# An attention block with a gated mixture layer on one core: the first tile's chain re-ordered, and the last unit's queries taken in wide pieces

## The chip, the cores and the metric

The kernel runs on one core of a Trainium2 chip. The metric is the device time of one execution in microseconds (us). The core's engines run side by side and wait for each other by semaphores: TensorE (PE in the profile; PEld is its weight load), VectorE (DVE), ScalarE (ACT), GpSimd (POOL) and SyncE (SP, which here issues nearly all DMAs).

## The reference

All tensors are float32; x is (2, 1024, 512).

```python
xn = (x - mean(x)) / sqrt(var(x) + 1e-5)
q, k, v = xn @ Wq.T + bq, xn @ Wk.T + bk, xn @ Wv.T + bv      # 32 heads of 16
att = softmax(where(causal, q k^T / 4, -inf))
s = (att @ v) @ Wo.T + bo
logits = xn @ W_gate.T                                        # 8 experts, the best 2 kept
h = (xn @ A^T) * route_w                                      # 8 experts of rank 16
g = silu(xn @ W_base.T + b_base + delta(h, B))
out = x + s * g
```

## The kernel before, in words

**Units and steps.** Attention is cut into 16 units (b, oc, c): a batch b of 2, a group oc of 8 heads of 4, a chunk c of 512 queries of 2. A unit is cut into steps. One step computes 512 columns of scores for four heads at a time: `scores(n)` (L1382) writes two PSUM tiles `s`, one for each pair of heads; two `exp` activations on ACT (L1391) write `pt`; `masked(n)` multiplies the pieces on the causal diagonal by `causal` on DVE; and `values(n)` (L1427) multiplies `pt` with v into the PSUM tiles `av0` and `av1` (`par` 0 and 1, four heads each). A step's pieces are tuples (par, key tile, first query, width, column). There are two `s` tiles of each pair's size in all, so scores(n+1) of a pair wait until the `exp` of that pair in step n has read them. A unit with c = 0 has 5 steps, one with c = 1 has 13, so there are 144 steps; the last unit (1, 3, 1) has steps 131 to 143.

**Order on PE.** For each n PE gets scores(n), values(n-1), and then `fill(n)`: a share of all other matrix work. That work is counted in units of MM = 0.853 us, one pass of 512 columns. The tasks are projections of q and k, of v, the gate and the output (as blocks with seven products instead of eight: `qk_blocks_task`, `block_task`), and routing. All go through the helper `matmul` (L221). The block products are `q` and `p`; the last chunk's output is done plainly as `po` by `whole_task` (4 MM, query tiles 0 to 2), `most_task` (3 MM) and `rest_task` (1 MM) for query tile 3.

**How much a step gets.** `fill(n)` sets `share`: an even part of what is left, or more if a task's due step asks for it. It takes units until the unit's end would pass the share: in an ordinary step it stops when what was taken plus 1/8 MM reaches the share, in a step with a causal piece when it plus 1/2 MM does. Before, the even part aims at step 136 with 16 MM kept for after it (`begin = len(plan) - 8`, `last_work`).

**PSUM for other work.** All projections and all transposes share a pool of two PSUM tiles (`mm_tile`); a new one waits until all readers of an older one are done. Two more hold av.

**The last unit before.** Its query tiles of 128 are done one after the other: `last_steps` lists, for each tile t and each par, all key tiles, and groups these 128-wide pieces by four. A tile's sums are copied (`avs`) as soon as it is through, transposed (`post_tile`, L936, PSUM tile `pt_o`), divided by the softmax's sums on DVE (`rc_last`, `olast`), transposed back (`turn_last`, L966, `pt_y`) and copied to `oT` by ACT (L967). Both transposes go through a list `late`, whose entries PE gets at the end of a fill. Then `whole_task` can run. After step 143: one unit of tile 2's `po`, `pt_o` of par 1 of tile 3, tile 2's last unit, `pt_y` of tile 3, `rest_task`. The DVE operations of `finish_tile` (`y`), of the range test (`fine`) and of the final flag (`count`, `sound`) follow. All engines read `sound` at the very end (`values_load`) to decide on a fallback.

**The first tile chain.** `first_task` handles the first 512 tokens in four tiles of 128: DVE statistics, POOL power, DVE normalization (`x`), four PE transposes (`pt_x`, L320), an ACT copy to `xnT` (L323), and projections `project_first` of q (`pq_first`) and k (`pk_first`, L331). Before it, 12 matmuls on `ident` (L170, `warm`) run, which POOL makes.

Of the kernel before, what the change touches and what calls it, by code (L numbers as in the profile page):

```python
# [80 lines left out]
def direct(ctx, tc, sound, x, wq, wk, wv, wo, wb, wa, wg, wB, bq, bk, bv, bo, bb, out):  # L81
# [81 lines left out]
            nc.sync.dma_start(out=dst, in_=src)  # L163


    ident = cst.tile([P, P], F32, name="ident")
    make_identity(nc, ident)
    warm = ps_mm.tile([P, D], F32, tag="mm", name="warm")
    for n in range(4 * WARM):
        nc.tensor.matmul(  # L170
            warm[:, n % 4 * P : n % 4 * P + P], lhsT=ident, rhs=ident, start=True, stop=True
        )
    b_sb = cst.tile([P, 2 * KC], F32, name="b_sb")
    bq_sb, bk_sb = b_sb[:, 0:KC], b_sb[:, KC : 2 * KC]
# [28 lines left out]
    rc_last = cst.tile([P, 2, TT, 4], F32, name="rc_last")  # L203

    MM = 0.853
    TR = 0.11

# [98 lines left out]
    def first_task():  # L308

        xnT = sb.tile([P, KC, C], F32, tag="xnT", bufs=3, name="xnT_0_0")  # L310
        qT = sb.tile([P, 2, C], F32, tag="qT", bufs=3, name="qT_0_0_0")
        kT = sb.tile([P, C], F32, tag="kT", bufs=4, name="kT_0_0_0")
        xnTs[0, 0], qTs[0, 0, 0], kTs[0, 0, 0] = xnT, qT, kT
        pq = ps_av.tile([P, C], F32, tag="av", name="pq_first")
        pk = ps_av.tile([P, C], F32, tag="av", name="pk_first")

        def turn(t):
            pt = mm_tile("pt_x")
            for k in range(KC):
                nc.tensor.transpose(  # L320
                    pt[:, k * P : (k + 1) * P], first[t][:, k * P : (k + 1) * P], ident
                )
            nc.scalar.copy(  # L323
                xnT[:, :, t * P : (t + 1) * P], pt.rearrange("p (k t) -> p k t", k=KC)
            )
            turned_at[0, 0] = now[0] - 5

        def project_first(ps, w, t):
            cols = slice(t * P, (t + 1) * P)
            for k in range(KC):  # L330
                nc.tensor.matmul(  # L331
                    ps[:, cols], lhsT=w[:, k, :], rhs=xnT[:, k, cols], start=k == 0, stop=k == KC - 1
                )

        def queries(par):
            ve.tensor_scalar(
                qT[:, par], pq, bq_sb[:, 0:1], half[:, par : par + 1], ALU.add, ALU.mult
            )

        def keys(t0, t1):  # L340
            cols = slice(t0 * P, t1 * P)
            nc.scalar.activation(kT[:, cols], pk[:, cols], AF.Identity, bias=bk_sb[:, 0:1])

        def transform(t, s):
            normalize(first[t : t + 1], *s)
            turn(t)

        s0 = yield from statistics(first[0 : 1])
        s1 = yield from statistics(first[1 : 2])
        transform(0, s0)  # L350
        b_ps = mm_tile("b_ps")[:, 0 : 2 * KC]
        nc.tensor.transpose(b_ps, b_rows, ident[0 : 2 * KC, 0 : 2 * KC])
        nc.scalar.copy(b_sb, b_ps)
        s2 = yield from statistics(first[2 : 3])
        transform(1, s1)
        project_first(pq, wqks[0][:, 0:KC], 0)
        s3 = yield from statistics(first[3 : 4])
        transform(2, s2)
        project_first(pk, wqks[0][:, KC:], 0)
        transform(3, s3)  # L360
        room["x"] += 1
        keys(0, 1)
        project_first(pq, wqks[0][:, 0:KC], 1)
        project_first(pq, wqks[0][:, 0:KC], 2)
        project_first(pq, wqks[0][:, 0:KC], TT - 1)
        queries(0)
        queries(1)
        for par in range(2):
            ve.tensor_scalar(bq_half[:, par], bq_sb, half[:, par : par + 1], None, ALU.mult)
        ve.tensor_tensor(b_less, bq_sb, bk_sb, ALU.subtract)  # L370
        project_first(pk, wqks[0][:, KC:], 1)
        yield 6 * MM
        project_first(pk, wqks[0][:, KC:], 2)
        project_first(pk, wqks[0][:, KC:], 3)
        keys(1, TT)
        yield 2 * MM
# [552 lines left out]
        later.append((n + 4 + wait, collect))  # L929
        later.append((n + 6 + wait, finish))  # L930

    def post_tile(b, oc, c, t, pars, avs):

        pt2 = mm_tile("pt_o")[:, 0 : 2 * P].rearrange("p (a s r) -> p a s r", a=2, s=4)
        for a in pars:
            nc.tensor.transpose(  # L936
                pt2[:, a].rearrange("p s r -> p (s r)"), avs[:, a * P : a * P + P], ident
            )
        if not last_out:
            last_out.append(sb.tile([P, TT, P], F32, tag="hw", bufs=1, name="olast"))  # L940
        rc = rc_last[:, :, t]
        heads = last_out[0][:, t].rearrange("p (s a d) -> p a s d", s=4, a=2)
        for a in pars:
            ve.reciprocal(rc[:, a], pt2[:, a, :, HD - a])
            ve.tensor_tensor(
                heads[:, a],
                pt2[:, a, :, HD * a : HD * a + HD],
                rc[:, a].unsqueeze(2).to_broadcast([P, 4, HD]),
                ALU.mult,
            )  # L950
            posted.append(t)

    posts, posted, later, patient, last_out = {}, [], [], [], []

    def project_out(po, b, c, t, k0, k1):
        for k in range(k0, k1):
# [4 lines left out]
            if k < k1 - 1:  # L961
                yield

    def turn_last(b, c, t, turned):
        pt = mm_tile("pt_y")[:, 0:P]
        nc.tensor.transpose(pt, last_out[0][:, t], ident)  # L966
        nc.scalar.copy(oTs[b, c][:, KC - 1, t * P : t * P + P], pt)  # L967
# [27 lines left out]

    def whole_task(b, c, t, hold=0):

        turned = []
        yield lambda: turn_last(b, c, t, turned), TR
        while not turned or normalized(b, c) < KC - 1:  # L1000
            yield WAIT
        while now[0] < hold:
            yield WAIT
# [15 lines left out]

    def rest_task(b, c, t):  # L1020

        turned = []
        list(last_in_range())
        yield lambda: turn_last(b, c, t, turned), TR
        while not turned:
            yield WAIT
        po = mm_tile("po")
        matmul(
# [45 lines left out]

    def last_steps(c):

        k0 = c * TT
        pieces = []
        for t in range(TT):
            for par in range(2):  # L1080
                for kt in [k0 + t] + list(range(k0 + t)):
                    pieces.append((par, kt, t * P, P, len(pieces) % 4 * P))
        return [pieces[n : n + 4] for n in range(0, len(pieces), 4)]

    units = [(b, oc, c) for b in range(NB) for oc in range(KC) for c in range(NC)]

# [79 lines left out]
    for b in range(NB):  # L1166
        for c in range(NC):
# [61 lines left out]
                lambda u=(b, c, "h"): now[0] > turned_at.get(u, now[0]) + 2,  # L1229
            )  # L1230
            if (b, c) != (NB - 1, NC - 1):
                by = min(len(plan) - 3, done + (21 if c else 19 if b else 30))
                stage(
                    out_task, ("out", b, c), by, 14 * MM, {"x": 1}, [("g", b, c)],
                    lambda b=b, c=c: normalized(b, c) == KC and (b, c) in g_tiles, {"x": 1},
# [1 line left out]
            else:  # L1237
# [8 lines left out]
                for t in range(TT - 1):  # L1246
# [2 lines left out]
                    Task(  # L1249
                        len(plan) + 9 if last_but_one else len(plan) - 1,  # L1250
                        whole_task(b, c, t, len(plan) - 1 if last_but_one else 0),
                        4 * MM + TR, after=before, ready=lambda t=t: posted.count(t) == 2,
                    )
                Task(
                    len(plan), most_task(b, c, TT - 1), 3 * MM, after=before,
                    ready=lambda b=b, c=c: normalized(b, c) == KC - 1,
                )
                Task(
                    len(plan) + 1, rest_task(b, c, TT - 1), MM + TR, after=before,
                    ready=lambda: posted.count(TT - 1) == 2,  # L1260
                )

# [3 lines left out]
        task.due = staged[k].due - int(staged[k].cost / 1.7) + 1 if k else -9  # L1266
    tasks.sort(key=lambda x: x.due)
    total = sum(x.cost for x in tasks)
    last_work = 16 * MM + 4 * TR
    spent = 0.0  # L1270
    late, active = [], []
    SV = 2.08
# [25 lines left out]
    def fill(n):  # L1298
# [5 lines left out]
        causal_here = within and mask_time(n)  # L1304
        for x in tasks:
            x.waiting = False

        begin = len(plan) - 8
        even = (total - spent) / max(1, len(plan) - n)
        if n == len(plan) - 1:  # L1310
            even = 2 * MM
        share = spent + (min(even, (total - last_work - spent) / (begin - n)) if n < begin else even)
        if n >= 12:

            left = 0.0
            for x in tasks:
                left += x.left
                if x.due > n:
                    share = max(share, spent + left / (x.due - n))
        while True:  # L1320
# [19 lines left out]
            if cost is None or cost is WAIT:  # L1340
                task.waiting = True
                active.clear()
            elif isinstance(cost, tuple):
                late.append((n, cost[0]))
                spent += cost[1]
            else:
                spent += cost
        ve.ready = 0.0
# [15 lines left out]
            x.waiting = said is WAIT  # L1364
        clock[0] = begins
        issue_parts()
        for _ in range(1 if active else 2):
            if late and (min(x[0] for x in late) <= n or not within):
                turn_late()

    avs_now, avs_last = {}, {}

    def scores(n):
        (b, oc, c), pieces, _, _ = plan[n]
# [38 lines left out]
    def values(n, pt):  # L1413
        (b, oc, c), pieces, is_first, is_last = plan[n]
        if is_first:
            avs_now.clear()
        for par, kt, q0, w, col in pieces:
            start = par not in avs_now
            if start:
                avs_now[par] = ps_av.tile([P, C], F32, tag="av", name=f"av{par}")  # L1420
            stop = is_last
            if (b, oc, c) == units[-1]:
                start = kt * P == c * C + q0
                stop = kt * P == c * C + q0 - P
            for s in range(4):
                h = 8 * oc + 2 * s + par
                nc.tensor.matmul(  # L1427
# [4 lines left out]
                    stop=stop,  # L1432
                )
        ve.ready = clock[0] + 2.0
        if (b, oc, c) == units[-1]:
            for par, kt, q0, _, _ in pieces:
                t = q0 // P
                if kt * P != c * C + q0 - P or not (par or t == TT - 1):
                    continue

                pars = [par] if t == TT - 1 else [0, 1]
                if t not in avs_last:
                    avs_last[t] = sb.tile([P, C], F32, tag="avs", name="avs")
                avs = avs_last[t]
                for p in pars:
                    ve.tensor_copy(avs[:, p * P : p * P + P], avs_now[p][:, q0 : q0 + P])
                late.append((n + 2, lambda a=(b, oc, c, t, pars, avs): post_tile(*a)))
        elif is_last:
            ve.tensor_copy(outputs(b, c)[:, oc], avs_now[0])
            avs = sb.tile([P, C], F32, tag="avs", name="avs")  # L1450
# [18 lines left out]
    third = next(x for x in tasks if x.begun)  # L1469
    third.step()  # L1470
    turn_late()
    while late or tasks:
        fill(last + 99)


# [460 lines left out]
```

## Time and profile before

| what | us |
|---|---|
| median of 3 runs | 602.25 (602.09 to 602.46) |
| the profiled execution's own time | 601.72 |
| its span, first to last instruction | 599.9 |
| PE busy in it | 588.0 (98%) |
| DVE busy | 392.1 |
| ACT busy | 319.3 |
| mean granted TensorE clock | 0.996 |
| first scores (step 0) start | 14.86 |
| last unit's first scores (step 131) | 537.42 |
| last `av` of the kernel, start | 587.79 |
| `sound` written, start | 594.27 |

The span is what the hardware profiler recorded; the execution's own time holds 1.82 us around it. In a timeline row the numbers are the start, the duration of the merged group, and in brackets the engine's idle time before it with the operation that ended it; `x8` counts records, and a float32 matmul leaves two. Because a matmul's end is modelled, differences between starts are a better measure than durations.

### The profile page before, as it was taken

What the parts mean: (1) busy time and instruction counts of PE and PEld (TensorE: products, weight loads), DVE (VectorE), ACT (ScalarE), POOL (GpSimd) and SP (SyncE); (2) the same over time, 40 slices, a digit from 0 to 9 for tenths busy, and PEclk for the clock granted to TensorE, in tenths of its full rate; (3) what the DMA queues carried; (4) which work ended last, traced back from release to release, by engine and by line L of the source; (5) the groups of instructions that cost most, each with busy time, mean ns of one, the idle gap of its engine ahead of it and who ended that gap; (6) DMA issues with size and microseconds to landing.
All of it is one profiled execution on the core that took longest, in us unless ns stands there. A gap on an engine that the chain in (4) does not pass through costs nothing.

```text
span 599.9 us, 19389 instructions
## 1 busy us (share of the span) xinstructions
PE 588.0 (98%) x8615; PEld 286.9 (48%) x8615; DVE 392.1 (65%) x831; ACT 319.3 (53%) x368; POOL 9.2 (2%) x26
## 2 busy tenths in 40 slices
PE   8999999999999999999999999999999999999995
PEld 7335344544445544444356544453444444457562
DVE  4546787287399857666487866664557865877532
ACT  2445454656555566556655454555565565565451
POOL 2000000000001000000000000000000000000000
PEclk9999999999999999999999999999999999999998
DMA  8524374247102535234132064440121023411101
GB/s 271 135 66 146 116 262 147 64 148 205 31 4 66 180 101 149 70 108 126 43 116 78 23 175 116 141 125 6 37 72 56 6 58 102 150 55 41 47 30 42
DMA packets 57932, 58.71 MB, mean 98 GB/s; under 512 B 8312, under 2 KB 49280, under 8 KB 57456
## 3 DMA queue, kind: packets, MB, share of 16 engines
q1 hardware_dynamic: 57824, 57.38, 31.0%
q8 instruction: 70, 1.15, 0.8%
q14 instruction: 22, 0.18, 0.1%
q10 hardware_dynamic: 16, 0.00, 0.0%
HBM read 43.24 MB, written 14.12 MB: 96 GB/s over the span
## 4 chain that ended last, share of the span: by engine, by line
PE 95%; DVE 2%; ACT 1%; DMA 0%; issue 0%; DVEq 0%
PE s L1382 25%; PE av L1427 23%; PE p L221 21%; PE q L221 13%; PE ph L221 3%; PE pv L221 2%; PE po L221 2%; PE pk L221 1%; PE pq L221 1%; ACT pt L1391 1%; PE pq_first L331 1%; PE h L221 1%; DVE x L55 0%; PE pk_first L331 0%; DMA x<-in_x_dram 0%; DVE y L55 0%
## 5 line engine op out<-in xcount | busy, mean ns | idle before, releaser
L1391 ACT ACTIVATE pt<-s 128x1024 f32<-128x1024 f32 x288 | 279.1, 1021 | 228.5 <-PE s L1382 228.5
L1382 PE MATMUL s<-qT,kT 32*128 32x512 f32 (+3 forms) x1824 | 166.1, 464 | 0.4 <-ACT pt L1391 0.3
L1427 PE MATMUL av<-pt,v 128*32 128x512 f32 (+3 forms) x1824 | 154.4, 443 | 0.3 <-PE s L1382 0.2
L55 DVE TENSOR_TENSOR pt<-pt,causal 128x512 f32<-128x512 f32 (+1 forms) x166 | 91.7, 567 | 72.0 <-ACT pt L1391 71.6
L1382 PEld LDWEIGHTS s<-qT,kT 32*128 32x128 f32 x1824 | 73.3, 184 | 66.5 <-issue 46.3
L1427 PEld LDWEIGHTS av<-pt,v 128*32 128x32 f32 x1824 | 43.3, 109 | 89.5 <-issue 58.3
L221 PE MATMUL p<-wt,asum 128*32 128x256 f32 x960 | 58.4, 379 | 0.0
L221 PE MATMUL q<-asum,wqk 128*32 128x256 f32 x832 | 50.6, 379 | 0.0
L221 PEld LDWEIGHTS p<-wt,asum 128*32 128x32 f32 x960 | 31.1, 110 | 26.4 <-issue 9.9
L221 PE MATMUL q<-xnT,wqk 128*32 128x256 f32 x624 | 40.0, 379 | 0.0
L221 PEld LDWEIGHTS q<-asum,wqk 128*32 128x32 f32 x832 | 27.0, 110 | 25.0 <-issue 8.4
L221 PEld LDWEIGHTS q<-xnT,wqk 128*32 128x32 f32 x624 | 20.9, 110 | 18.7 <-issue 5.1
L55 DVE TENSOR_TENSOR g<-p,g 128x512 f32<-128x512 f32 x28 | 18.9, 686 | 15.3 <-PE p L221 15.1
L221 PE MATMUL p<-w,xnT 128*32 128x256 f32 x448 | 27.3, 379 | 0.0
L55 DVE SCALAR_TENSOR_TENSOR kT<-q,kT 128x256 f32<-128x256 f32 x39 | 16.4, 422 | 14.1 <-PE q L221 13.5
L55 DVE TENSOR_TENSOR v<-p,v 128x512 f32<-128x512 f32 x21 | 14.1, 687 | 11.2 <-PE p L221 11.2
L221 PE MATMUL p<-w,asum 128*32 128x256 f32 x320 | 20.0, 379 | 0.0
L55 DVE TENSOR_TENSOR x<-p,x 128x512 f32<-128x512 f32 x21 | 14.2, 687 | 8.9 <-PE p L221 8.9
L221 PEld LDWEIGHTS p<-w,xnT 128*32 128x32 f32 x448 | 14.5, 110 | 11.1 <-issue 3.3
L748 ACT ACTIVATE sg<-g 128x512 f32<-128x512 f32 x16 | 10.0, 630 | 17.5 <-DVE g L55 17.5
L708 ACT ACTIVATE qT<-qT,half 128x512 f32<-128x512 f32 x26 | 18.8, 722 | 0.4
L221 PE MATMUL ph<-wag_sb,xnT 128*32 128x136 f32 x512 | 17.2, 279 | 0.0
(132 smaller groups left out, 479.8 us busy)
## 6 DMA issues: line engine op xcount, KB each, us to landing
wt<-kept SPq DMA_DIRECT2D x40, 256.0 KB
x<-in_x_dram SPq DMA_DIRECT2D x16, 256.0 KB
scr<-sq SPq DMA_DIRECT2D x6, 512.0 KB
xnT<-scr SPq DMA_DIRECT2D x24, 128.0 KB
w<-in_wb_dram SPq DMA_DIRECT2D x12, 256.0 KB
xr<-in_x_dram SPq DMA_DIRECT2D x12, 256.0 KB
out_dram<-x SPq DMA_DIRECT2D x12, 256.0 KB
w<-in_wv_dram SPq DMA_DIRECT2D x9, 256.0 KB
```

The source lines that it names most:

```text
L55: return getattr(self.engine, name)(*args, **named)
L221: nc.tensor.matmul(o[j : j + 32], lhsT=lhsT[:, j : j + 32] if len(lhsT.shape) == 2 else lhsT[:, j // 32], rhs=rhs, start=start, stop=stop,)
L331: nc.tensor.matmul(ps[:, cols], lhsT=w[:, k, :], rhs=xnT[:, k, cols], start=k == 0, stop=k == KC - 1)
L708: nc.scalar.activation(qT[:, par], qT[:, 0], AF.Copy, scale=half[:, par : par + 1])
L748: nc.scalar.activation(sg, g(i, j), AF.Tanh, scale=0.5)
L1382: nc.tensor.matmul(ss[s // 2][:, s % 2, col : col + w], lhsT=kT[rows, kt % TT * P : kt % TT * P + P], rhs=qTs[b, oc, c][rows, par, q0 : q0 ...
L1391: nc.scalar.activation(pt[:, 2 * pair : 2 * pair + 2], ss[pair], AF.Exp, scale=0.25)
L1427: nc.tensor.matmul(avs_now[par][32 * s : 32 * s + 32, q0 : q0 + w], lhsT=vs[b, kt][:, h * VS - HD * par : h * VS - HD * par + HP], rhs=pt[ ...
```

## The change

Five things change.

1. The warm-up matmuls read a tile `blank` that DVE clears, not `ident`.
2. In `first_task` the second tile is normalized and transposed before the statistics of the third; three projections (q of tile 0, k of tile 0, q of tile 1) stand between it and the third and fourth tiles' transposes.
3. `last_steps`: query tiles 0 to 2 of the last unit are done together, 384 wide, in the first nine steps (131 to 139), filled up to 512 columns with pieces of 128; tile 3 takes steps 140 and 141 (par 0) and 142 and 143 (par 1). The sums of tiles 0 to 2 are closed at step 139 and copied as two 384-wide copies; their three `pt_o` go to the list `late`.
4. `turn_last` is no longer a step of its task through `late`, but is put in a list `turns` by `post_tile`, and PE gets it at the start of the next fill.
5. The planner: from 8 steps before the last unit up to step 141 the even part is what is left without `whole_task` and `rest_task`, divided by the steps up to 141; `begin` and `last_work` are 141 and 13 MM; the due steps of the last block output and of `most_task` move; in the last unit two entries of `late` can go out in a fill also while a task is under way.

```diff
+    blank = cst.tile([P, P], F32, name="blank")
+    ve.memset(blank, 0.0)
...
-            warm[:, n % 4 * P : n % 4 * P + P], lhsT=ident, rhs=ident, start=True, stop=True
+            warm[:, n % 4 * P : n % 4 * P + P], lhsT=blank, rhs=blank, start=True, stop=True
...
+        transform(1, s1)
         s2 = yield from statistics(first[2 : 3])
-        transform(1, s1)
+        s3 = yield from statistics(first[3 : 4])
         project_first(pq, wqks[0][:, 0:KC], 0)
-        s3 = yield from statistics(first[3 : 4])
+        project_first(pk, wqks[0][:, KC:], 0)
+        project_first(pq, wqks[0][:, 0:KC], 1)
         transform(2, s2)
-        project_first(pk, wqks[0][:, KC:], 0)
         transform(3, s3)
         room["x"] += 1
         keys(0, 1)
-        project_first(pq, wqks[0][:, 0:KC], 1)
         project_first(pq, wqks[0][:, 0:KC], 2)
...
+        if posted.count(t) == 2:
+            turns.append((now[0] + 1, lambda: turn_last(b, c, t)))
...
-        turned = []
-        yield lambda: turn_last(b, c, t, turned), TR
-        while not turned or normalized(b, c) < KC - 1:
+        while t not in turned or normalized(b, c) < KC - 1:
             yield WAIT
...
-        k0 = c * TT
-        pieces = []
-        for t in range(TT):
-            for par in range(2):
-                for kt in [k0 + t] + list(range(k0 + t)):
-                    pieces.append((par, kt, t * P, P, len(pieces) % 4 * P))
-        return [pieces[n : n + 4] for n in range(0, len(pieces), 4)]
+        k0, w = c * TT, C - P
+        steps = []
+        for par in range(2):
+            for kt in range(0, k0, TT):
+                for i in range(TT - 1):
+                    steps.append([(par, kt + i, 0, w, 0), (par, kt + TT - 1, i * P, P, w)])
+        steps += [[(par, k0, 0, w, 0), (par, k0 + 2, 2 * P, P, w)] for par in range(2)]
+        steps.append([(par, k0 + 1, P, 2 * P, 2 * P * par) for par in range(2)])
+        keys = [k0 + TT - 1] + list(range(k0 + TT - 1))
+        pieces = [(par, kt, w, P, i % 4 * P) for par in range(2) for i, kt in enumerate(keys)]
+        return steps + [pieces[n : n + 4] for n in range(0, len(pieces), 4)]
...
-                by = min(len(plan) - 3, done + (21 if c else 19 if b else 30))
+                by = min(len(plan) - 3, done + (21 if c else 22 if b else 30))
...
-                    len(plan), most_task(b, c, TT - 1), 3 * MM, after=before,
+                    len(plan) - 1, most_task(b, c, TT - 1), 3 * MM, after=before + 4,
...
-    last_work = 16 * MM + 4 * TR
+    last_work = 13 * MM
...
+        for turn in [turn for turn in turns if turn[0] <= n]:
+            turns.remove(turn)
+            turn[1]()
+
+        begin = len(plan) - 3
         even = (total - spent) / max(1, len(plan) - n)
         if n == len(plan) - 1:
             even = 2 * MM
-        share = spent + (min(even, (total - last_work - spent) / (begin - n)) if n < begin else even)
+        if n >= starts[units[-1]] - 8 and n < begin:
+            even = sum(x.left for x in tasks if x.steps.__name__ not in ("whole_task", "rest_task"))
+            even /= begin - n
+        elif n < begin:
+            even = min(even, (total - last_work - spent) / (begin - n))
+        share = spent + even
...
-        for _ in range(1 if active else 2):
+        for _ in range(1 if active and n < starts[units[-1]] else 2):
             if late and (min(x[0] for x in late) <= n or not within):
                 turn_late()
...
+            if len(firsts) == 2:
+                for t in range(TT - 1):
+                    of = {par: firsts[par][:, t * P : t * P + P] for par in range(2)}
+                    late.append((n + 1, lambda a=(b, oc, c, t, of): post_tile(*a)))
+                firsts.clear()
...
-    while late or tasks:
+    while late or turns or tasks:
         fill(last + 99)
```

More of the change, by code (lines that the diff above doesn't have):

```diff
@@ L205, in direct @@
     MM = 0.853
-    TR = 0.11
     WAIT = object()
@@ L930, in post, with post_tile @@
         later.append((n + 6 + wait, finish))
-    def post_tile(b, oc, c, t, pars, avs):
+    def post_tile(b, oc, c, t, avs):
         pt2 = mm_tile("pt_o")[:, 0 : 2 * P].rearrange("p (a s r) -> p a s r", a=2, s=4)
[L935 to L938, printed above, removed]
+        for a in avs:
+            nc.tensor.transpose(pt2[:, a].rearrange("p s r -> p (s r)"), avs[a], ident)
         if not last_out:
@@ L942, in post_tile @@
         heads = last_out[0][:, t].rearrange("p (s a d) -> p a s d", s=4, a=2)
-        for a in pars:
+        for a in avs:
             ve.reciprocal(rc[:, a], pt2[:, a, :, HD - a])
@@ L951, in post_tile @@
             posted.append(t)
-    posts, posted, later, patient, last_out = {}, [], [], [], []
+        if posted.count(t) == 2:
+            turns.append((now[0] + 1, lambda: turn_last(b, c, t)))
+    turns, turned, posts, posted, later, patient, last_out = [], [], {}, [], [], [], []
     def project_out(po, b, c, t, k0, k1):
@@ L962, in project_out, with turn_last @@
                 yield
-    def turn_last(b, c, t, turned):
+    def turn_last(b, c, t):
         pt = mm_tile("pt_y")[:, 0:P]
@@ L1020, in rest_task @@
     def rest_task(b, c, t):
-        turned = []
         list(last_in_range())
-        yield lambda: turn_last(b, c, t, turned), TR
-        while not turned:
+        while t not in turned:
             yield WAIT
@@ L1251, in direct @@
                         whole_task(b, c, t, len(plan) - 1 if last_but_one else 0),
-                        4 * MM + TR, after=before, ready=lambda t=t: posted.count(t) == 2,
+                        4 * MM, after=before, ready=lambda t=t: posted.count(t) == 2,
                     )
                 Task(
-                    len(plan), most_task(b, c, TT - 1), 3 * MM, after=before,
+                    len(plan) - 1, most_task(b, c, TT - 1), 3 * MM, after=before + 4,
                     ready=lambda b=b, c=c: normalized(b, c) == KC - 1,
@@ L1258, in direct @@
                 Task(
-                    len(plan) + 1, rest_task(b, c, TT - 1), MM + TR, after=before,
+                    len(plan) + 1, rest_task(b, c, TT - 1), MM, after=before,
                     ready=lambda: posted.count(TT - 1) == 2,
@@ L1306, in fill @@
             x.waiting = False
-        begin = len(plan) - 8
+        for turn in [turn for turn in turns if turn[0] <= n]:
+            turns.remove(turn)
+            turn[1]()
+        begin = len(plan) - 3
         even = (total - spent) / max(1, len(plan) - n)
@@ L1316, in fill @@
             for x in tasks:
+                if x.steps.__name__ in ("whole_task", "rest_task"):
+                    continue
                 left += x.left
@@ L1342, in fill @@
                 active.clear()
-            elif isinstance(cost, tuple):
-                late.append((n, cost[0]))
-                spent += cost[1]
             else:
@@ L1366, in fill @@
         issue_parts()
-        for _ in range(1 if active else 2):
+        for _ in range(1 if active and n < starts[units[-1]] else 2):
             if late and (min(x[0] for x in late) <= n or not within):
                 turn_late()
-    avs_now, avs_last = {}, {}
+    avs_now, avs_last, firsts, last_pieces = {}, [], {}, {}
+    for n in range(starts[units[-1]], len(plan)):
+        for par, kt, q0, _, _ in plan[n][1]:
+            last_pieces.setdefault((par, q0 == C - P), []).append((n, kt, q0))
     def scores(n):
@@ L1416, in values @@
             avs_now.clear()
+        ends = (b, oc, c) == units[-1]
+        closed = []
         for par, kt, q0, w, col in pieces:
@@ L1421, in values @@
             stop = is_last
-            if (b, oc, c) == units[-1]:
-                start = kt * P == c * C + q0
-                stop = kt * P == c * C + q0 - P
+            if ends:
+                group = par, q0 == C - P
+                start, stop = last_pieces[group][0] == (n, kt, q0), last_pieces[group][-1] == (n, kt, q0)
+                if stop:
+                    closed.append(group)
             for s in range(4):
@@ L1434, in values @@
         ve.ready = clock[0] + 2.0
[L1435 to L1447, printed above, removed]
+        if ends:
+            for par, late_ones in closed:
+                o = avs_now[par]
+                if late_ones:
+                    if not avs_last:
+                        avs_last.append(sb.tile([P, 2, P], F32, tag="rb", bufs=1, name="avs"))
+                    avs = avs_last[0][:, par]
+                    ve.tensor_copy(avs, o[:, C - P : C])
+                    late.append((n + 2, lambda a=(b, oc, c, TT - 1, {par: avs}): post_tile(*a)))
+                else:
+                    avs = sb.tile([P, C], F32, tag="avs", name="avs")
+                    ve.tensor_copy(avs[:, 0 : C - P], o[:, 0 : C - P])
+                    firsts[par] = avs
+            if len(firsts) == 2:
[3 more added lines that the diff above has]
+                firsts.clear()
         elif is_last:
```

## Prediction

> **What bounds the kernel now.** First the page's head: PE is busy for 588.0 of 599.9 us. Then the view of busy time by stretches, which says where the other 11.9 us lie (columns: PE's, PEld's, DVE's, ACT's, POOL's busy us and instructions, granted clock, DMA).
>
> ```profile
> span 599.9 us, 19389 instructions
> PE 588.0 (98%) x8615; PEld 286.9 (48%) x8615; DVE 392.1 (65%) x831; ACT 319.3 (53%) x368; POOL 9.2 (2%) x26
> ```
> ```profile
> 0.00:14.86 14.86, 12.29 (x89) 11.58 (x89) 6.99 (x20) 3.96 (x7) 4.48 (x17) 1.00 0.89 272
> ...
> 200.00:300.00 100.00, 100.00 (x1380) 44.04 (x1372) 64.04 (x129) 56.81 (x62) 1.43 (x3) 1.00 0.35 104
> ...
> 537.42:588.69 51.27, 49.60 (x1094) 32.87 (x1094) 28.43 (x69) 26.08 (x30) 0.00 (x0) 1.00 0.14 45
> 588.69:599.90 11.21, 3.84 (x36) 0.84 (x28) 3.93 (x11) 0.27 (x1) 0.00 (x0) 0.79 0.16 56
> ```
>
> PE has 2.57 us idle before step 0, 1.67 in the last unit, 7.37 behind the last `av`, and next to nothing between. PE work is only moved here, so the change can win these idle times, or add new ones. Third, PE's waits from 537.4 us on, and fourth, the timeline, which shows a wait that the list misses:
>
> ```profile
> PE pt_y L966 <- DVE olast L55: 1.0, 1, 1.0
> PE pt_o L936 <- DVE y L55: 0.4, 1, 0.4
> ```
> ```profile
> 534.48 1.15 PE L1382 MATMUL s<-qT,kT 32*128 32x256 f32 x16
> ...
> 536.45 1.05 PE L221 MATMUL p<-wt,asum 128*32 128x256 f32 x16
> 537.42 1.39 PE L1382 MATMUL s<-qT,kT 32*128 32x128 f32 x32
> 538.75 1.07 PE L1427 MATMUL av<-pt,v 128*32 128x256 f32 x16
> ```
>
> Step 130 took one unit of other work and lasted 2.94 us; the next `s` then took 1.33 instead of 1.10 until `av`. The reason is ACT: `exp` starts 1.2 after `s`, its two halves take 1.94, so the second pair of the next `s` is free only about 3.2 after. It counts as busy, since the first pair runs meanwhile. Step 132 to 133 repeats it (544.45 to 545.76). With two units a step lasts 3.80 and nothing is held. The barest case is step 142, with no unit:
>
> ```profile
> 581.73 1.94 ACT L1391 ACTIVATE pt<-s 128x1024 f32<-128x1024 f32 x2 [2.20 <-PE s L1382]
> 582.63 0.33 PE L966 MATMUL pt_y<-ident,olast 128*128 128x128 f32 x1
> 582.89 0.49 PE L1382 MATMUL s<-qT,kT 32*128 32x128 f32 x4
> 583.55 0.27 ACT L967 COPY oT<-pt_y 128x128 f32<-128x128 f32 x1
> 583.72 1.16 PE L1382 MATMUL s<-qT,kT 32*128 32x128 f32 x28 [0.33 <-ACT pt L1391]
> ```
>
> Read two things: that `s` lasts 1.91 until `av` (584.80), 0.81 too long; and ACT copies a `pt_y` only behind the `exp` of its step, 0.92 after the transpose began.
>
> **Removed in the last unit.** The wait before `pt_y` in step 136 (0.97), the one before `pt_o` in 138 (0.36), the held `s` of 143 (0.81), of 131 and 133 (0.22 each): 2.58. Nine steps in wide pieces: narrow `s` and `av` take 1.10 and 0.90 from start to start, wide ones 1.08 and 0.89 (steps 123 and 124), so 9 x 0.03 = 0.27. Together 2.85.
>
> A rule speaks to this last term: the Trainium skill, "Perfetto Trace Analysis", section "Matmuls", says larger matmuls are more efficient, when possible; here four pieces cost 0.03 us a step more than one, so on this trace the rule is worth 0.27 us, and it does not lead.
>
> **Added: the fills.** I worked the planner's rule by hand. For steps 129 to 136 before it gives 2, 1, 2, 1, 2, 2, 1, 0 units, as the trace has. With the change the steps up to 122 keep their fills (the even part stays between 1.5 and 2 units, or due steps lead). At 123 there are 39 units left (2 of a gate, 7 of q and k, 14 of an output block, 16 of the last chunk, counted from the rows behind 507.91), 26 without `whole_task` and `rest_task`: 26/18 = 1.44 a step. Steps 123 to 140 get 1, 2, 2, 2, 2, 1, 1, 1, 2, 2, 2, 2, 1, 1, 1, 1, 1, 1 (123 is on a tie and may get 2). Nothing more may go before 141, as tiles 0 to 2 are transposed only then: 141 gets 13/3, rounded up to 5, then 142 gets 3 and 143 gets 2.
>
> One-unit steps hold the next `s`. A held `s` starts its step late, so that after it one unit fits; I count every second one: 124, 129, 136, 138, 140 at 0.22, and 130 at 0.36, as the two `qT` copies (1.48, after step 128's `exp`) push its predecessor's `exp` back. That is 1.46. Bounds: 0.66 (three) and 2.6 (eleven at 0.22, and 0.2). In step 138 DVE runs the output block's last add and two finishing operations (2.0) before the masks; `av` waits about 0.1.
>
> **Added: step 140.** `most_task`'s last unit leaves its `po` in one PSUM slot, the first `pt_o` takes the other, the second waits until DVE has read `po`. DVE is in order: two copies (0.48 each, between 0.24 for 128 columns and 0.61 for 512), two masks after the `exp`, then `y`. The same chain ran before from the second mask at 566.95 to `pt_o` at 568.03, 1.08. The second mask comes about 3.0 after `s`, so 4.1; PE is there at 1.1 + 0.9 + 0.97 + 0.37 = 3.3. Wait 0.8 (bounds 0, if `po` is read early, and 2.2, if it gets the other slot and needs the first tile's readers too).
>
> **Added: step 141.** Two `pt_y` now go out at the start of the fill, 2.1 after `s`, end at 2.65 and hold both slots. ACT copies the first at 1.2 + 1.82 = 3.02 behind its `exp`, done 3.29; tile 0's `po` starts at 3.34. Wait 0.7 (0 to 0.9). A third `pt_o` then follows `y` closely, 0.05. Fills of 5, 3 and 2 hold nothing else; DVE's and SP's three output writes there have the fills' 4 and more us as cover.
>
> Sum to the last `av`: 1.46 + 0.1 + 0.8 + 0.7 + 0.05 - 2.85 = **+0.25**.
>
> **The tail.** Columns as before:
>
> ```profile
> 589.66 0.33 PE L936 MATMUL pt_o<-ident,avs 128*128 128x128 f32 x1
> 589.92 1.07 PE L221 MATMUL po<-wo,oT 128*32 128x512 f32 x8
> 590.92 0.33 PE L966 MATMUL pt_y<-ident,olast 128*128 128x128 f32 x1
> 591.05 0.69 DVE L55 SCALAR_TENSOR_TENSOR y<-po,g 128x512 f32<-128x512 f32 x1 [0.58 <-PE po L221]
> ...
> 592.73 0.69 DVE L55 SCALAR_TENSOR_TENSOR y<-po,g 128x512 f32<-128x512 f32 x1
> ```
>
> Tile 2's last unit of `po` fills PE between `pt_o` and `pt_y`, while DVE divides. The new list runs at the start of the fill, so `pt_y` comes ahead of that unit. It waits for `olast` (590.48) to about 590.6, ends at 590.88; the unit starts there, 0.96 later than 589.92. Behind it DVE does `y`, `y`, `fine`, `fine`, the last `y`, `y`, `count`, `sound` back to back, the first at 592.0 instead of 591.05. The gain of an earlier `pt_y` (0.3) meets a `po` that DVE can't read yet. **+0.95** (bounds 0.3, were the last `y` free to overtake, and 1.1). Behind `sound` 5.5 us follow as before.
>
> **The start.** `warm` needs `blank`, a DVE clear that no row shows (POOL's clear of that size took 0.20; bounds 0 and 0.7, a 512-wide DVE operation); its cover is DVE's wait for x until 3.61. `warm` is off the path either way: the first `pt_x` waits for DVE's `x` (6.23). The second `pt_x` started at 7.78, held by its normalization (7.10 to 7.64); now that could run at 6.63, when POOL is done (6.59), but the PSUM slot is busy until ACT's copies end (7.57). So 0.15 is won. Then 0.46 + 1.0 + 2 x 0.89 of PE work lead to the third `pt_x` at 10.87, the fourth ends at 11.77, and q of tile 2 needs ACT's copy of tile 2, done 1.26 after its `pt_x` began (9.24 to 10.50): 12.15. PE waits 0.4, where before q of tile 1 was the cover. Step 0 starts at 15.1, **+0.2** (bounds -0.15, no wait, and +0.4, nothing won). If k's weights, now read at 9.1 instead of 9.7, land late, it grows.
>
> A rule speaks against the earlier warm-up: the granted clock reads 1.00 throughout, but `warm` records come at 7 per us until 4.4 us and at 14 per us from 4.9. The Trainium skill, "TensorE: Matmul & The Clock Gate", Part 1, says that PE runs at half rate again after an idle window of some 3.4 us. A `warm` that ends 0.4 earlier leaves PE mostly idle from 5.5 to 7.6; by the rule that is too short to matter, and the sum by it is the same. No row here shows a fall-back.
>
> **Sum.** 0.25 + 0.95 + 0.2 = +1.4 us. The profiled execution would take 601.72 + 1.4 = 603.1; the runs' median lies 0.53 above it, so the forecast is 602.25 + 1.4 = **603.65**. A measurement can tell about 0.2%, 1.2 us, from no change.
>
> **Rivals.**
> - *The two slot waits stay away* (140 and 141), because DVE and ACT reach `po` and `pt_y` before PE asks: it decides from 0.8 us earlier `exp`. Then 1.4 - 1.5 = -0.1, **602.15**, not slower. For it: step 141 of before had `pt_o` right behind a `po` without a wait (580.15). Against: there the other slot was free.
> - *More waits than counted*: every one-unit step holds (5 x 0.22 = 1.1), or the second `pt_o` waits for the first one's readers (1.35 more). **604.75 to 605.0**. For it: 3.2 is over 2.94 in every such step. Against: `exp` of the held step 131 started at 538.67, before `av`.
> - *Nothing new waits*: `exp` is ready ahead of PE in all of 124 to 141, -2.85 + 0.95 + 0.2 = -1.7, **600.55**. For it: no list of waits shows more than 0.4 for ACT. Against: 131, 133 and 143.
>
> **How the numbers follow.** Forecast 0.50, its own range 603.0 to 604.5, 0.14 of it under +1.2; two waits away 0.16; more waits 0.21; nothing waits 0.13. Slower: 0.36 + 0.21 = 0.57. Same: 0.14 + 0.16 = 0.30. Faster: 0.13. The range leaves out the last rival and the far end of the second: 601.3 to 605.1.
>
> **What would show it.** Right: `s` of 1.3 us after one-unit steps; PE idle before the second `pt_o` (DVE `y`) and before tile 0's `po` (ACT `oT`); `pt_y` ahead of the last but one `po`, and `sound` 6.5 us, not 5.6, after the last `av` ends (588.69 here); step 0 after 15.0. Wrong: fills of another pattern, a full last unit without these waits, or a changed middle.

## The result, and the profile after

The changed kernel takes 604.08 us (median of 8 runs, 603.52 to 604.75) where the kernel before took 602.38 on the same chip (602.09 to 604.08): a ratio of 1.0025, with a 95% interval from 1.0015 to 1.0034, so 0.9 to 2.0 us more. The forecast was 1.4 us more (603.65). A ratio here is the one on record for the two sets of runs; it is not the quotient of the two medians, from which it differs by up to 0.001.

The profiled execution took 604.41 us, with a span of 602.6. Line numbers have moved by 1 to 17. First the head of the page of the changed kernel, to be set beside that of before.

```profile
span 602.6 us, 18802 instructions
PE 589.4 (98%) x8327; PEld 283.5 (47%) x8327; DVE 391.7 (65%) x822; ACT 319.0 (53%) x368; POOL 9.0 (1%) x26
```

PE has 288 fewer records, which is what the wide pieces save, and yet its busy time grew by 1.4, of it 1.1 before step 0 (13.38 and 12.29): a slow PE counts as busy, as does one whose second half of a group waits. Its idle time is 13.2 us instead of 11.9. The view by stretches says where (columns: PE's, PEld's, DVE's, ACT's, POOL's busy time and instructions, granted clock, DMA share, GB/s). The stretches are: before step 0, from the last unit's first scores to the end of the last `av`, and behind it.

```profile
0.00:15.34 15.34, 13.38 (x90) 12.69 (x90) 7.25 (x21) 3.86 (x7) 4.25 (x17) 1.00 0.83 260
...
536.79:590.27 53.48, 51.92 (x854) 28.89 (x854) 29.64 (x62) 25.70 (x29) 0.00 (x0) 1.00 0.13 43
590.27:602.60 12.33, 3.68 (x36) 0.94 (x28) 3.89 (x11) 0.27 (x1) 0.00 (x0) 0.78 0.14 50
```

The last unit still has 1.56 us of idle PE (1.67 before), so the old waits went and as many came. The tail has 8.65 instead of 7.37. PE's waits from 505 us on name them:

```profile
PE pn L1030 <- DVE fine L55: 1.1, 1, 1.1
PE po L222 <- ACT oT L968: 0.8, 1, 0.8
PE pt_o L937 <- DVE y L55: 0.8, 1, 0.8
PE pt_y L967 <- DVE olast L55: 0.6, 1, 0.6
```

The second and third are the two waits forecast for steps 141 and 140; the other two lie in the tail. The timeline of PE shows each in its place (the first row, of ACT, is the `exp` that the `s` behind it waits for):

```profile
553.25 1.94 ACT L1403 ACTIVATE pt<-s 128x1024 f32<-128x1024 f32 x2 [1.86 <-PE s L1394]
553.98 1.05 PE L222 MATMUL p<-w,asum 128*32 128x256 f32 x16
554.96 1.42 PE L1394 MATMUL s<-qT,kT 32*128 32x384 f32 x16
556.31 1.07 PE L1444 MATMUL av<-pt,v 128*32 128x384 f32 x16
...
570.46 0.44 PE L937 MATMUL pt_o<-ident,avs 128*128 128x128 f32 x2
571.65 0.44 PE L937 MATMUL pt_o<-ident,avs 128*128 128x128 f32 x2 [0.76 <-DVE y L55]
...
574.14 0.44 PE L967 MATMUL pt_y<-ident,olast 128*128 128x128 f32 x2
575.38 4.50 PE L222 MATMUL po<-wo,oT 128*32 128x512 f32 x40 [0.80 <-ACT oT L968]
...
591.25 0.33 PE L937 MATMUL pt_o<-ident,avs 128*128 128x128 f32 x1
592.20 0.30 PE L967 MATMUL pt_y<-ident,olast 128*128 128x128 f32 x1 [0.62 <-DVE olast L55]
592.43 1.92 PE L222 MATMUL po<-wo,oT 128*32 128x512 f32 x16
595.45 0.22 PE L1030 MATMUL pn<-fine,ones 128*1 128x34 f32 x2 [1.09 <-DVE fine L55]
```

A held `s` is read from starts: behind one unit of `p`, 554.96 to 556.31 is 1.35, where 1.08 would do; PE's list of waits does not have it. The `exp` of the step before ends at 555.19, and the records of the second half of this `s` start at 555.25. In the tail, `pt_y` now stands and waits ahead of the `po` that had covered its wait.

By stages, in the profiled executions (us). The last `av` ends where the first `po` of the tail starts.

| stage | before | after | difference | forecast |
|---|---|---|---|---|
| to step 0 | 14.86 | 15.34 | +0.48 | +0.2 |
| step 0 to 123 | 493.05 | 493.71 | +0.66 | 0 |
| step 123 to the last `av`'s end | 80.78 | 81.22 | +0.44 | +0.25 |
| from there to `sound` | 5.58 | 6.49 | +0.91 | +0.95 |

The 0.66 in the middle lies in step 15 alone (4.10 and 4.76 us), though the change doesn't touch it: DVE's reciprocal waited 0.58 for a DMA (`dens`), and DVE's masks and `av` came behind. Among the twelve profiles of this document it shows in four, three times with the changed start and once with the old one (4.66 to 4.99), and not in the other eight (4.08 to 4.16), of which four have the changed start. It comes and goes with the same code, so it is taken as chance in a profile and no part of the change. Behind `sound` another 0.2 was added; the twelve profiles have 5.6 to 6.1 us there, whatever their tail, and before had the least. So two profiled executions alone would have given 2.7 us, for a difference that the runs put at 1.7.

### The profile page after: what moved, and what is told of

The parts are those of the page before. It is cut to its first block, busy times and chain, and to the rows that moved or that the text cites. A ratio compares the mean times of both kernels' runs of the same rounds, so it can differ in the third digit from the quotient of the medians.

```text
span 602.6 us, 18802 instructions
## 1 busy us (share of the span) xinstructions
PE 589.4 (98%) x8327; PEld 283.5 (47%) x8327; DVE 391.7 (65%) x822; ACT 319.0 (53%) x368; POOL 9.0 (1%) x26
## 4 chain that ended last, share of the span: by engine, by line
PE 93%; DVE 3%; DMA 2%; issue 1%; ACT 0%; SPq 0%; ACTq 0%; DVEq 0%
PE s L1394 25%; PE av L1444 23%; PE p L222 20%; PE q L222 13%; PE ph L222 2%; PE pv L222 2%; PE po L222 2%; DMA kept<-wqk 1%; PE pq L222 1%; PE pk L222 1%; PE warm L172 1%; DMA dens<-den 1%; DVE wqk L55 1%; PE pq_first L332 1%; PE h L222 1%
## 5 line engine op out<-in xcount | busy, mean ns | idle before, releaser
L1444 PEld LDWEIGHTS av<-pt,v 128*32 128x32 f32 x1680 | 39.8, 109 | 93.6 <-issue 61.4
```

Of the source, the lines that this page charges most:

```text
L1444: nc.tensor.matmul(avs_now[par][32 * s : 32 * s + 32, q0 : q0 + w], lhsT=vs[b, kt][:, h * VS - HD * par : h * VS - HD * par + HP], rhs=pt[ ...
```

## The experiments

The theory: the changed last unit costs all of it, 1.2 of the 1.4 us, as two waits for PSUM, held `s` and a tail order, against 2.85 removed. The rivals: the start costs it, or the last unit's waits go into slack elsewhere. All ten kernels were timed against the kernel before on the same chip; a ratio of 0.002 is 1.2 us. Three chips were used, so two experiments are compared by their ratios to before.

**The start alone.** The kernel before with the cleared tile, the warm-up on it, and the new order of `first_task`:

```diff
+    blank = cst.tile([P, P], F32, name="blank")
+    ve.memset(blank, 0.0)
...
+        transform(1, s1)
         s2 = yield from statistics(first[2 : 3])
-        transform(1, s1)
+        s3 = yield from statistics(first[3 : 4])
```

> The kernel before with the start of the change alone (cleared tile for the warm-up, new order of the first chain). Theory of the prediction: PE waits for ACT's copy of tile 2, the warm-up costs nothing, so step 0 starts at about 15.1 us and the time is 0.2 us above before. Second theory, from the profile after: the warm-up on zeros runs at the slow rate to its end and holds back the first transposes too, step 0 at 15.3 and 0.5 above before. Rival: the start costs nothing, step 0 at 14.9 and a time like before; the whole loss is in the last unit and behind it.

602.38 against 602.18: 0.9993 (0.9984 to 1.0003). No price of the start shows; a price of 0.2 us at most fits (the medians alone would say 0.2 more). Its profile, the slowest of its eleven runs, has a warm-up that is slow to its end and step 0 at 15.56; its last two stages take 80.78 and 5.58 us, as before, so the start leaves them alone.

**The last unit alone.** The changed kernel with its start undone (warm-up on `ident`, old order).

```diff
-        transform(1, s1)
         s2 = yield from statistics(first[2 : 3])
-        s3 = yield from statistics(first[3 : 4])
+        transform(1, s1)
...
-            warm[:, n % 4 * P : n % 4 * P + P], lhsT=blank, rhs=blank, start=True, stop=True
+            warm[:, n % 4 * P : n % 4 * P + P], lhsT=ident, rhs=ident, start=True, stop=True
```

> The changed kernel with the start as it was before (warm-up on ident, old order of the first chain). Theory of the prediction: the last unit's waits come to 0.25 and the tail to 0.95, so the time is 1.2 us above before, with sound 6.5 us after the last av ends. Rival: the loss is the start's alone and the time is that of before.

603.63 against 602.18: 1.0020 (1.0012 to 1.0029), that is 0.7 to 1.7 us. Its trace has 81.22 and 6.48 us in the last two stages. The theory holds: the last unit and its tail carry the loss.

**The tail's order.** In the changed kernel, tile 2's unit is put back ahead of tile 3's `pt_y`.

```diff
     turn_late()
+    third.step()
     while late or turns or tasks:
```

> The changed kernel; behind the last step the fourth unit of tile 2's po goes to PE ahead of tile 3's pt_y, as before the change. Theory: DVE's last operations start 0.95 us earlier after the last av, the time falls by 0.9 us against the changed kernel, about 0.8 above before. Rival: the last unit of tile 3's po, not DVE, sets the end, and the time stays within 0.2 of the changed kernel.

602.77 against 602.18: 1.0006 (0.9997 to 1.0015), by the ratios some 1.1 us less than the whole change, whose interval it touches. PE's timeline:

```profile
592.11 0.33 PE L967 MATMUL pt_y<-ident,olast 128*128 128x128 f32 x1
592.80 1.07 PE L222 MATMUL po<-wo,oT 128*32 128x512 f32 x8 [0.35 <-ACT oT L968]
```

A unit of `po` ahead of these rows (591.11 to 592.11) fills PE while DVE divides, `pt_y` no longer waits, and the stage to `sound` is 5.59, as before. The one line gives the term for the tail back in full.

**What the warm-up reads.** The changed kernel with ones in `blank`.

```diff
-    ve.memset(blank, 0.0)
+    ve.memset(blank, 1.0)
```

> The changed kernel with the cleared tile set to 1.0 instead of 0.0, so that only the data of the warm-up differ. If zeros are what kept the warm-up at the slow rate, its records reach 14 per us some 3.3 us after its start as they did on ident before, the first transposes start at 6.1 instead of 6.4, and step 0 some 0.2 to 0.3 earlier than 15.34. Rival: the moment of the change of rate has nothing to do with the data, and this run shows the slow rate to the end as well, or another moment, with the time of the changed kernel within 0.2.

603.89 against 602.18: 1.0021 (1.0013 to 1.0030). The zeros are not what made the warm-up slow to its end in the profile of the changed kernel: with ones it is slow to its end too (below).

**One PSUM tile for two `pt_o`.** In the changed kernel the transposes of tiles 0 and 1 go into one PSUM tile, those of tile 2 a step later.

```diff
-        pt2 = mm_tile("pt_o")[:, 0 : 2 * P].rearrange("p (a s r) -> p a s r", a=2, s=4)
-        for a in avs:
-            nc.tensor.transpose(pt2[:, a].rearrange("p s r -> p (s r)"), avs[a], ident)
+        ps = mm_tile("pt_o").rearrange("p (t a s r) -> p t a s r", t=2, a=2, s=4)
+        for k, (t, avs) in enumerate(of.items()):
+            for a in avs:
+                nc.tensor.transpose(ps[:, k, a].rearrange("p s r -> p (s r)"), avs[a], ident)
```

> The changed kernel, but the transposes of tiles 0 and 1 in step 140 write one PSUM tile (they fit in one bank), so that no second slot is needed and tile 2's come at the end of fill 141. Theory: PE's wait of 0.8 us before the second pt_o goes, step 141 starts 3.9 after step 140 instead of 4.64, and the time falls by 0.7 against the changed kernel. Rival: DVE's chain behind it (y, two sums, the divisions) is what counts, the wait moves to pt_y in step 141 and the time stays within 0.2.

602.92 against 602.73: 1.0004 (0.9995 to 1.0013), by the ratios some 1.3 us less than the whole change. PE's timeline:

```profile
569.44 0.66 PE L938 MATMUL pt_o<-ident,avs 128*128 128x128 f32 x4
...
572.84 0.30 PE L969 MATMUL pt_y<-ident,olast 128*128 128x128 f32 x1 [0.38 <-DVE olast L55]
573.38 4.50 PE L222 MATMUL po<-wo,oT 128*32 128x512 f32 x40 [0.23 <-ACT oT L970]
```

The four transposes run without a gap and step 140 takes 3.66 instead of 4.64. The wait for DVE's `y` was a wait for a PSUM tile and for nothing else. In step 141 a smaller wait for `olast` comes up, 0.38 and 0.23 instead of 0.80, so the stage from step 123 is 0.97 shorter, a little more than the wait taken away.

**One `pt_y` ahead of the fill.** In the changed kernel, of two due `pt_y` only the first goes out at the start of the fill, the other at its end.

```diff
-        for turn in [turn for turn in turns if turn[0] <= n]:
+        due_turns = [turn for turn in turns if turn[0] <= n]
+        for turn in due_turns[:1]:
...
+        for turn in due_turns[1:]:
+            turns.remove(turn)
+            turn[1]()
```

> The changed kernel, but a fill starts with one pt_y at most and a second one goes out at its end, so that in step 141 tile 0's po finds a free PSUM slot. Theory: PE's wait of 0.8 us for ACT's copy of oT goes, fill 141 takes 4 units and 142 takes 4, the time falls by 0.8 minus at most 0.1 against the changed kernel. Rival: po then waits for the slot's former reader on DVE, and the time stays within 0.2.

603.40 against 602.73: 1.0014 (1.0005 to 1.0023), by the ratios 0.7 us less than the whole change, but the intervals overlap; the gain rests on the trace. PE's timeline behind the first `pt_y`:

```profile
574.48 3.64 PE L222 MATMUL po<-wo,oT 128*32 128x512 f32 x32
578.06 0.33 PE L967 MATMUL pt_y<-ident,olast 128*128 128x128 f32 x1
578.74 0.44 PE L937 MATMUL pt_o<-ident,avs 128*128 128x128 f32 x2 [0.36 <-ACT oT L968]
```

`po` starts without a wait, so the cause of the 0.80 was the second `pt_y` in the other PSUM tile. But about half came back elsewhere: the `pt_o` behind now waits 0.36 for ACT's copy. The stage is 0.33 shorter, less than half of the 0.80. (Its step 0, at 16.11, came late by 0.9 for the DMA of the first weights, in this one execution.)

**All mended.** The last unit as changed, with the edits of the last two and of the tail's order together, and the start undone.

```diff
     turn_late()
+    third.step()
...
+        ps = mm_tile("pt_o").rearrange("p (t a s r) -> p t a s r", t=2, a=2, s=4)
...
+        for turn in due_turns[:1]:
```

> The changed kernel with all four: the start as it was before, po ahead of pt_y behind the last step, the shared PSUM tile in step 140, one pt_y at the start of a fill. What is left of the change is the wide pieces and the even spread. Theory: the waits removed (2.58) and the narrow pieces' 0.27 are won, the held steps (0.9 to 1.5 us of them by the two traces) are lost, so the time lies 1.3 to 1.9 us under before, about 600.7. Rival: the waits only move on to DVE or ACT, and the time is that of before within 0.5.

601.77 against 602.73: 0.9984 (0.9975 to 0.9993). That is 1.0 us faster than before (0.4 to 1.5) and beats both kernels. It is less than the 1.3 to 1.9 us expected, since the held `s` are all still there (1.6 us, step for step as in the changed kernel) and each mend leaves a smaller wait:

```profile
572.96 3.64 PE L220 MATMUL po<-wo,oT 128*32 128x512 f32 x32 [0.38 <-DVE olast L55]
...
577.22 0.44 PE L936 MATMUL pt_o<-ident,avs 128*128 128x128 f32 x2 [0.36 <-ACT oT L968]
```

Its stage from step 123 is 80.38, 0.40 under before, and its tail 5.59, as before. So the profile shows where 0.4 us of the 1.0 come from, the lower end of what the runs allow; the rest was not found. The shared tile alone has that stage at 80.25: one `pt_y` at the start of a fill gains nothing on top of it.

**The start's order, and the start on the mended kernel.** First the changed kernel with the old order of `first_task`, keeping the warm-up on `blank`; then the mended kernel with the changed start.

```diff
-        transform(1, s1)
         s2 = yield from statistics(first[2 : 3])
-        s3 = yield from statistics(first[3 : 4])
+        transform(1, s1)
```

> The changed kernel with the old order of the first chain, but the warm-up on the cleared tile, so that against the changed kernel only the order differs and against the run with the whole start undone only the warm-up. Theory of the prediction: the new order costs 0.2, the warm-up nothing, so this time is 0.2 under the changed kernel and equal to the run with the start undone, about 603.7. Rival from the other traces: the moment at which the warm-up reaches the fast rate varies from run to run and covers any such difference, and the three are equal within 0.4.

603.65 against 602.73: 1.0015 (1.0006 to 1.0024).

> The kernel with the last unit and tail mended (601.77 in its run), but with the changed start. The start's price is what is still open: its own runs against before and the runs with it undone lie within 0.1% of each other and of no change. Theory of the prediction: 0.2 us above the mended kernel's ratio to before (0.9984), so 0.9987. From the mean start of step 0 in the profiles (15.4 with the new order, 15.0 with the old): 0.4 above, 0.9991. Rival: the start costs nothing, 0.9984 or less.

601.69 against 602.62: 0.9984 (0.9975 to 0.9993), the very ratio with the old start. So no price of the start can be told from none: its three comparisons (alone on before; changed kernel with either order; mended kernel with either start) give -0.4, +0.6 and 0.0 us, and the changed kernel with its whole start undone +0.3, each with an interval that includes zero or overlaps the other kernel's.

**No warm-up.** The mended kernel with the old start, without the twelve warm-up products.

```diff
-    warm = ps_mm.tile([P, D], F32, tag="mm", name="warm")
-    for n in range(4 * WARM):
-        nc.tensor.matmul(
-            warm[:, n % 4 * P : n % 4 * P + P], lhsT=ident, rhs=ident, start=True, stop=True
-        )
```

> The mended kernel with the start as before, but with no warm-up matmuls at all (they compute nothing that is used). Theory: PE's rate doubles only some 3.3 to 5.5 us after PE's work begins, so the first transposes and projections run at the slow rate for that long and step 0 starts 1.5 to 3 us later than 15.1, with the time up by as much against 0.9984 of before. Rival: the rate rises by itself at 4.5 to 7 us whatever PE does, the first transpose at 6 is fast in most runs, and the time is unchanged within 0.3.

603.23 against 602.62: 1.0012 (1.0003 to 1.0021), by the ratios 1.7 us more than with the warm-up (the mended kernel with the changed start, on the same chip, has a median 1.5 lower). PE's timeline has step 0 at 16.68:

```profile
6.07 1.12 PE L314 MATMUL pt_x<-ident,x 128*128 128x128 f32 x4 [6.07 <-DVE x L55]
8.77 1.92 PE L325 MATMUL pq_first<-xnT,wqk 128*128 128x128 f32 x8
```

The first transposes and projections run at half rate (1.12 instead of 0.66 for four records, 1.92 instead of 1.06 for eight, by the same rows of before). PE changes its rate only at about 11.6 us, 5.5 us after PE's first work, so the rival, that the rate rises by itself at 4.5 to 7 us whatever PE does, is refuted. This is the largest effect of the start that any run showed.

## Why the prediction was right

*The last unit's terms held.* Fills from step 123 to 143 are, unit for unit, those worked out by hand (the tie at 123 fell to one). The wait before the second `pt_o` is 0.76 (forecast 0.8), the one before tile 0's `po` 0.80 (0.7), and a shared PSUM tile for the one and a later `pt_y` for the other take them away, so the causes named are the causes.

*Held `s`: the sum right, the pattern wrong.* I counted every second one-unit step, 1.46 in all with step 130. In fact eight of the ten one-unit steps (I had bounded them at eleven) hold the next `s`, by more or less: 0.28, 0.28 and 0.24 in steps 124, 129 and 130, nothing in 131, 0.27 in 136, 0.11 to 0.18 from 137 to 140, and nothing in 141. Together that is 1.6. In each of the eight the second half of `s` starts 0.05 or 0.06 us after the end of the `exp` of the step before, so ACT is the cause as foretold; no run took the held `s` away, so their price is read from the trace alone. A step that begins late makes the next hold smaller, but does not always take it away; that this came out at my sum is partly luck. The rival in which all of them hold was nearly right in the number and wrong in the size. The two small terms did not come: `av` did not wait for the masks in step 138 (0.1), nor the third `pt_o` (0.05).

*Removed.* The stage grew by 0.44. Taking 1.6 of held `s` and 1.56 of waits from it leaves -2.7, where I had -2.85. That is a remainder, not a measurement of its own, but the lists agree: the waits for `pt_y` in step 136, `pt_o` in 138 and `s` in 143 are gone. A wide step takes 1.08 and 0.89 from start to start, as reckoned. So the change lost in this stage because what it placed, 3.16, is more than what it took away.

*The tail* took 0.91 more (0.95). DVE's timeline of the changed kernel gives the reason as foretold, `y` coming later (593.57, where before had it at 591.05) and everything behind it back to back up to the last `y`:

```profile
593.57 0.69 DVE L55 SCALAR_TENSOR_TENSOR y<-po,g 128x512 f32<-128x512 f32 x1 [1.51 <-PE po L222]
...
595.22 0.68 DVE L55 SCALAR_TENSOR_TENSOR y<-po,g 128x512 f32<-128x512 f32 x1
```

*The start* is where the prediction had a step wrong: it called the warm-up off the path either way. The +0.48 of the profile lies outside the bounds given (-0.15 to +0.4), because there the warm-up is slow to its end, the first `pt_x` waits for it (6.40 instead of 6.23) and is partly slow too. Where the warm-up is over in time and no weights come late (tail order, shared tile, mended kernel with the changed start), the new order has step 0 at 14.98 to 15.05, 0.12 to 0.19 after before's, near the forecast of 0.2; the wait of q of tile 2 for ACT's copy is 0.24 wherever the new order ran, not 0.4. The runs show no price at all.

*The rivals.* That the two waits stay away, and that nothing waits, are refuted by the list of waits. That the second `pt_o` waits 1.35 more for the first one's readers did not come either (0.76). The whole, 0.44 and 0.91 from the profile and nothing certain from the start, is 1.35; the runs say 0.9 to 2.0, too wide to confirm the small terms one by one.

## What to carry to other kernels

When short transposes share a few PSUM tiles with long projections, count the tiles and their readers at every place to which a transpose is moved: the reader (DVE in order, or ACT behind its `exp`) sets when the next one may start (0.76 us here, gone once two tiles' transposes shared a PSUM tile). Here a long product beside a wait was worth more than the earlier start of what waits: one `po` moved ahead of a waiting `pt_y` won 0.9 us. Mending a wait uncovers the one under it, so the wait's length is no forecast of the gain unless the whole chain is worked out again (0.33 of 0.80 in one case here, 0.97 for a wait of 0.76 in another, and 0.84 for both mends together).

## What the runs showed of the hardware

The moment at which PE doubles its rate differs from execution to execution. PE's first rows of the changed kernel:

```profile
1.12 5.49 PE L172 MATMUL warm<-blank 128*128 128x128 f32 x24 [1.12 <-DVE blank L55]
6.40 0.78 PE L321 MATMUL pt_x<-ident,x 128*128 128x128 f32 x4
```

And of the mended kernel with the changed start, whose warm-up is the same and starts at the same time:

```profile
1.11 4.67 PE L172 MATMUL warm<-blank 128*128 128x128 f32 x24 [1.11 <-DVE blank L55]
```

In the first the 24 records are slow to the end, 5.3 us after the start, and the first transposes wait for them and are partly slow themselves; in the second the last records come at double rate. The operands don't decide it: slow to the end were zeros twice, ones once and `ident` once; faster before the end, zeros five times and `ident` twice. From the start of the warm-up to the change it took 3.2 us (before) to at least 5.9 us (ones in `blank`), and in the kernel without a warm-up 5.5 from the first work. The granted clock reads 1.00 throughout, so the rate must be read from the records: they start 0.21 us apart while PE is slow and 0.11 us apart behind the change. (The prediction's 7 and 14 per us count every record that reaches into a stretch; by their starts there are 4.7 and 9 per us.) The Trainium skill, "TensorE: Matmul & The Clock Gate", Part 1, puts the transition at around 4 us into sustained matmul work, give or take 0.5; these rows spread wider on both sides. No run here shows what sets the moment.
